# Keeping the last two steps' rows on chip and loading Toeplitz rows by halves, in a GRU, convolution and MoE kernel

## The chip, the cores and the metric

The kernel runs on one core of one Trainium2 chip. The metric is the device time of one execution in microseconds, as the median of several runs. The engines are named as in the profile: PE (TensorE, with PEld for its weight loads), DVE (VectorE), ACT (ScalarE), POOL (GpSimd), and SP (SyncE), whose work here is to issue DMAs. PEq, SPq, ACTq and POOLq are the queues in which an engine's instructions wait to be issued.

## The reference, cut to what matters

`x` is 128 x 64 x 512 (batch, steps, features), `cond` 128 x 512, all float32. Two layers change `x` one after the other:

```
# layer 0
h = cond
for t in range(64):                       # GRU over the 64 steps, state 512
    r, z = sigmoid(...), sigmoid(...)
    n = tanh(i_n + r * h_n)
    h = (1 - z) * n + z * h
    hs[:, t] = h
x = x + hs @ ternary(weight).T + bias     # BitLinear: sign matrix times one scale

# layer 1
w = cond[:, None, :]                      # 128 taps for each of the 512 features
y = depthwise_causal_conv(x, w) + b       # y[b, t, d] = sum over s <= t of x[b, s, d] * w[127 - (t - s), d]
y = moe(y) + shared_expert(y)             # 64 experts, top 6, plus a SwiGLU of width 704
x = x + y
```

Because the 64 steps are shorter than the 128 taps, the convolution of one feature `d` is a product of the 128 x 64 matrix of its inputs with a 64 x 64 triangular Toeplitz matrix of taps.

## The kernel before, in words

The work is written with a framework in which pools of tiles share on-chip memory. A new tile waits for whatever still uses the memory it takes. Each engine and each queue runs its instructions in the order in which the framework arranged them, and `tc.issue_after(i)` asks that what is issued in its block on the engine of `i` comes behind `i`.

**GRU stage (0 to 1405 us).** Step `t` runs 12 matmuls of 512 columns (L480) with the gates on DVE and ACT. Between them PE does the input gates two steps ahead (L326) and `ffn(t - 1)` (L398), the BitLinear product of the step before. `ffn` writes `x1` (L413), the row block of one output step, and stores it twice: into `x1c` (L415), the convolution's input in DRAM, arranged by feature, and into `out` (L428). The last two steps (`TAIL = 2`) are not stored into `x1c`; zeros stand there. Their part of the convolution, which concerns only the last two output steps, is computed on DVE by `tail_products` (L551) from `xl` (the two rows, loaded again from `out`, L546) and `tap` (the last two rows of `cond`), and added at L583. In steps 2 to 33 `toeplitz` (L129) writes the Toeplitz rows of 16 features at a time from the array `taps` into DRAM (`tzd`), each a window of 64 taps.

**Convolution stage (1405 to 1500 us).** It has 16 slices (`NSL`) of 32 features. For a slice, `load_piece` (L147) loads `xc` (1 MB: partitions are 2 feature halves x 64 steps) and two `tz` tiles of 256 KB (`load_toeplitz`, L141; one on SP's queue, one on ACT's for most slices). There are four buffers (`NCB`), so slice `n + 4` is loaded when slice `n` has been multiplied. `clear` (L118) zeroes on POOL the blocks of `tz` that belong to the other feature half. `conv_group` (L163) multiplies four features: `parts=2` splits the 128 batch rows in two halves of 64 columns of the array, `parts=1` takes all 128 at once. A slice has four groups. The four groups of slice 0 are issued early (L512 to L520), around the last transposes and the last `ffn`, into the memory banks psx, psy, psw, psz; the other slices use four banks psc. DVE adds the bias and writes `hid` (L571), 64 tiles of 128 x 512 that stay on chip, two instructions for a group. `hid` takes over the memory of the GRU stage's tiles. Rows 0 to 3 of `hid` are stored into the table `tab` (L590) in two portions, after slice 13 and after slice 15, because the next stage transposes them in place.

**First MoE block (from 1500 us).** The weights of the shared expert (`gw`, `swr`, `swg`, `swu`, L612 to L621) are loaded on SP's queue into the memory of the convolution's buffers. `put_rows` (L1007) stores further rows of `hid` into `tab`. `route(0)` (L940) transposes rows 0 to 3 on PE (L947), copies them back in place (L948) and computes the logits. `shared(0)` (L821) forms the sums `s1`, `s2` on DVE (L830, L831) and runs seven products for each block of 128 columns (L664) after Winograd's variant of Strassen's scheme; `prepare_shared(c)` (L627) makes the weights' sums that products 5 and 6 need (psz and y at L664). The rest of the time (1519 to 2697 us) goes to the other 15 blocks and to the routed experts.

Of the kernel before, what the change touches and what calls it, by code (L numbers as in the profile page):

```python
# [42 lines left out]
def adaln_ffn_kernel(  # L43
# [30 lines left out]
    tzd = dram.tile([2 * NSL, T, DS, T], F32, name="tzd")  # L74
# [23 lines left out]
    def load_rows(dst, src):  # L98

        nc.sync.dma_start(out=dst, in_=src.rearrange("(k p) n -> p k n", p=P))  # L100
# [9 lines left out]
    def conv_buffers(i):  # L110
        cv = conv.enter_context(
            tc.tile_pool(name=f"cv{i}", bufs=1, side="right", reuse_waits="tile")
        )
        tz = cv.tile([P, 2, DS, T], F32, name=f"tz{i}")
        tzs.append(tz)
        xcs.append(cv.tile([P, B, DS], F32, name=f"xc{i}"))

    def clear(i):  # L118
        for hf in range(2):
            nc.gpsimd.memset(tzs[i][hf * T : (hf + 1) * T, 1 - hf], 0.0)  # L120

# [6 lines left out]

    def toeplitz(q):  # L129

        i = nc.sync.dma_start(
            out=tzd[q],
            in_=bass.AP(taps.tensor, taps.offset + q * DS * 2 * T, [[1, T], [2 * T, DS], [1, T]]),
        )
        tc.keep_in_program_order(i)

        nc.sync.dma_start(
            out=x1c[q, :TAIL].rearrange("s (r b) e -> (s r) (b e)", r=8), in_=zrow[: 8 * TAIL, : B * DS // 8]
        )

    def load_toeplitz(sl):  # L141

        for hf, queue in enumerate((nc.sync, nc.sync if 2 <= sl < NCB else nc.scalar)):
            queue.dma_start(out=tzs[sl % NCB][hf * T : (hf + 1) * T, hf], in_=tzd[2 * sl + hf])

    TAIL = 2
    def load_piece(sl):  # L147
        load_toeplitz(sl)
        nc.sync.dma_start(
            out=xcs[sl % NCB], in_=x1c[2 * sl : 2 * sl + 2].rearrange("h s b e -> (h s) b e")  # L150
        )
# [11 lines left out]
    def conv_group(sl, g, ps, parts=2):  # L163


        ps = ps.rearrange("p (j h t) -> p j h t", j=4, h=2)
        for j in range(4):
            for r in range(parts):
                rows = slice(r * B // parts, (r + 1) * B // parts)
                i = nc.tensor.matmul(  # L170
                    ps[rows, j],
                    xcs[sl % NCB][:, rows, g * 4 + j],
                    tzs[sl % NCB][:, :, g * 4 + j, :],
                    start=True,
                    stop=True,
                )
        grouped.append(i)
        return ps
# [9 lines left out]
    with (  # L188
# [96 lines left out]
        gis = {}  # L285
# [112 lines left out]
        def ffn(t, pieces):  # L398
# [13 lines left out]
            x1 = io0.tile([P, D], F32, name="x1")  # L412
# [48 lines left out]
        for t in range(T):  # L461
# [9 lines left out]
            if t == T - TAIL:  # L471
                wi_.close()
                for i in range(2, NCB):
                    conv_buffers(i)
                    clear(i)
            ps_g = []
# [35 lines left out]
        early = [conv_group(0, 0, ps_gi.tile([P, D], F32, name="psx"), 1)]  # L512
        with tc.issue_after(grouped[-1].ins):
            turned = turned_up(h)
        early.append(conv_group(0, 1, ps_gi.tile([P, D], F32, name="psy"), 1))
# [3 lines left out]
        early.append(conv_group(0, 2, ps_gi.tile([P, D], F32, name="psw"), 1))  # L519
        early.append(conv_group(0, 3, ps_gi.tile([P, D], F32, name="psz")))  # L520
# [21 lines left out]


    tail = conv.enter_context(tc.tile_pool(name="tail", bufs=1, reuse_waits="tile"))
    xl = tail.tile([P, TAIL, D], F32, name="xl")
    nc.gpsimd.dma_start(out=xl, in_=out_t[T - TAIL :].rearrange("t b d -> b t d"))  # L546
    tap = tail.tile([P, TAIL, D], F32, name="tap")
    for j in range(TAIL):
        nc.gpsimd.dma_start(out=tap[:, j], in_=cond[B - 1 - j].partition_broadcast(P))
# [7 lines left out]

    cb_h = cb.rearrange("p (q h d) -> p q h d", h=2, d=DS)
    with tc.tile_pool(name="ps_c", bufs=4, space=PSUM) as ps_c:
        for sl in range(NSL):  # L560

            if sl >= NCB:
                load_piece(sl)
            for g in range(DS // 4):
                if early:
                    ps = early.pop(0)
                else:
                    ps = conv_group(sl, g, ps_c.tile([P, D], F32, name="psc"))
                d = slice(g * 4, g * 4 + 4)
                for th in range(2):  # L570
                    nc.vector.tensor_tensor(  # L571
                        hids[th][:, :, 2 * DS * sl : 2 * DS * (sl + 1)].rearrange(
                            "p t (h d) -> p t h d", h=2
                        )[:, :, :, d],
                        ps[:, :, :, th * TH : (th + 1) * TH].rearrange("p j h t -> p t h j"),
                        cb_h[:, sl, :, d].unsqueeze(1).to_broadcast([P, TH, 2, 4]),
                        ALU.add,
                    )
            if sl >= NCB:
                if sl == NCB:  # L580
                    tail_products()
                d = slice(0 if sl == NCB else 2 * DS * sl, 2 * DS * (sl + 1))
                nc.vector.tensor_add(  # L583
                    hids[1][:, TH - TAIL :, d], hids[1][:, TH - TAIL :, d], xl[:, :, d]
                )

            if sl in (NSL - 3, NSL - 1):
                d = slice(0, 2 * DS * (NSL - 2)) if sl == NSL - 3 else slice(2 * DS * (NSL - 2), D)
                for t in range(4):
                    nc.sync.dma_start(out=tab_t[t, :, d], in_=hid(t)[:, d])  # L590
# [30 lines left out]
    load_rows(swu, sw_up[:, : full * P])  # L621
# [5 lines left out]
    def prepare_shared(c):  # L627
# [8 lines left out]
        nc.vector.tensor_sub(t4, w21, t2)  # L636

    NB = 4
    NI = T // NB
# [10 lines left out]
    def winograd(n, accs, lhs, rhs, k0=0):  # L650
# [11 lines left out]
        for k in range(HK):  # L662
            r = rhs(k)
            nc.tensor.matmul(  # L664
# [6 lines left out]
            )  # L671
        return ps
# [148 lines left out]
    def shared(i, sums=None):  # L821
# [8 lines left out]
        nc.vector.tensor_add(s1, x21, x22)  # L830
        nc.vector.tensor_sub(s2, s1, x11)  # L831
        if i == 0:
            prepare_shared(0)
# [13 lines left out]
        for p in range(2):  # L847
            sg = sh.tile([P, QT], F32, name=f"g{p + 1}")
            nc.scalar.activation(sg[rest:], gu[:rest, p * QT : (p + 1) * QT], AF.Silu)
            for j in range(2):  # L850
                nc.vector.tensor_mul(
                    aTr[j * rest : (j + 1) * rest, p],
                    sg[rest:, j * P : (j + 1) * P],
                    gu[rest:, p * QT + j * P : p * QT + (j + 1) * P],
                )
# [7 lines left out]
        for c in range(full):  # L863
            cur = Block(c, ops, aT)
            for n in (1, 6, 7, 3, 2, 4, 5):
                which = prev if n == 3 else cur
                if which:
                    which.product(n)
# [65 lines left out]
    with (  # L934
# [5 lines left out]
        def route(i):  # L940


            for j in range(NB):
                t = i * NB + j
                ps = ps_t1.tile([P, KD, P], F32, name="pst1")
                for k in range(KD):
                    nc.tensor.transpose(ps[:, k, :], hid(t)[:, k * P : (k + 1) * P], ident)  # L947
                nc.vector.tensor_copy(hid(t).rearrange("p (k b) -> p k b", k=KD), ps)  # L948
# [58 lines left out]
        def put_rows(i):  # L1007
            if i < NI:
                for t in range(i * NB, i * NB + NB):
                    nc.sync.dma_start(out=tab_t[t, :, :D], in_=hid(t))  # L1010
# [9 lines left out]
        for _ in range(NB + 1):  # L1020
            next(ahead)
        for i in range(NI // 2):
# [3 lines left out]
            def routing():  # L1026
                if i == 0:
                    yield from ahead
                for r in (2 * i + 1, 2 * i + 2):
                    if r < NI:  # L1030
                        yield from route(r)
# [3 lines left out]
            for n, _ in enumerate(shared(i)):  # L1035
                if done * PIECES <= n * 16:
                    next(routing_, None)
# [384 lines left out]
```

## Time and profile before

| what | value |
|---|---|
| median of 3 runs | 2700.56 us (2699.63 to 2701.82) |
| profiled execution | 2699.08 us |
| its span in the profile | 2697.0 us |
| PE busy in the span | 2647.6 us (98%) |
| mean granted clock of PE | 0.997 |
| GRU stage | 0 to 1405 us, PE busy 1394.08 |
| convolution | 1405 to 1500 us, PE busy 72.63 |
| first MoE block, to its regular pace | 1500 to 1519 us, PE busy 14.95 |
| rest | 1519 to 2697 us, PE busy 1165.96 |

The profile is one execution. Its waits view sums the idle time of an engine by what ended it. The timeline merges instructions of one kind in order of time and gives in brackets the idle time before them. The windows view gives for a stretch of time the busy time and number of instructions of PE, PEld, DVE, ACT and POOL, then the clock granted to PE (1.00 is full speed), the share of the DMA engines that is busy, and the rate in GB/s. A float32 matmul appears as two records.

### The profile page before, as it was taken

How to read it: one execution, taken by the hardware profiler on the slowest of the kernel's cores; microseconds unless marked ns; L12 is line 12 of the kernel's file. 1: busy time of each engine (PE TensorE's matmuls, PEld its weight loads, DVE VectorE, ACT ScalarE, POOL GpSimd, SP SyncE). 2: the span in 40 equal slices, each digit the busy share in tenths (PEclk: the TensorE clock that was granted, in tenths of full speed). 3: DMA queues.
4: the chain of work that ended last, by engine and by line, in shares of the span. 5: the costliest groups of instructions: out<-in, count | busy, mean ns of one | idle time of the engine just before them, and what ended most of it. 6: DMA issues, size and time to landing. Idle time of an engine off the chain costs nothing. (4 is left out here: it accounts for less than half of the span.)

```text
span 2697.0 us, 31139 instructions
## 1 busy us (share of the span) xinstructions
PE 2647.6 (98%) x11935; PEld 1825.2 (68%) x11935; DVE 1414.2 (52%) x3148; ACT 426.1 (16%) x794; POOL 425.2 (16%) x475
## 2 busy tenths in 40 slices
PE   8999999999999999999997899999999999999999
PEld 5666666666666666666667766777777666666667
DVE  6555555555555555555546655555665333433334
ACT  1111111111111111111110222222221111111111
POOL 2111111111111111111110000000001222222220
PEclk9999999999999999999999999999999999999999
DMA  5333223232222222322249631222255999998962
GB/s 191 74 61 72 61 62 63 55 63 55 63 47 57 50 50 51 66 51 43 44 98 274 244 117 22 39 56 57 62 151 166 288 306 287 303 317 267 297 186 47
DMA packets 459588, 328.04 MB, mean 122 GB/s; under 512 B 312304, under 2 KB 378864, under 8 KB 457264
## 3 DMA queue, kind: packets, MB, share of 16 engines
q1 hardware_dynamic: 432336, 255.52, 34.0%
q0 software_dynamic: 25984, 66.86, 10.5%
q10 hardware_dynamic: 1120, 3.67, 0.6%
q8 instruction: 94, 1.54, 0.2%
q14 instruction: 54, 0.44, 0.1%
HBM read 239.73 MB, written 94.65 MB: 124 GB/s over the span
## 5 line engine op out<-in xcount | busy, mean ns | idle before, releaser
L480 PE MATMUL psgh<-whh,hT 128*128 128x512 f32 x1536 | 674.5, 595 | 0.7 <-ACT hT L387 0.7
L480 PEld LDWEIGHTS psgh<-whh,hT 128*128 128x128 f32 x1536 | 286.8, 190 | 349.8 <-issue 336.0
L326 PE MATMUL psx<-wih,xp 128*128 128x256 f32 x768 | 198.8, 381 | 6.2 <-DMA wih<-in_w_ih_dram 6.2
L208 POOL DMA_DIRECT2D xn<-in_x_dram x61 | 33.9, 555 | 838.2 <-DVE x L413 826.6
L326 PEld LDWEIGHTS psx<-wih,xp 128*128 128x128 f32 x768 | 143.9, 191 | 25.8 <-issue 6.2
L490 DVE TENSOR_TENSOR n<-psgh,bhn 128x512 f32<-128x512 f32 x64 | 44.3, 692 | 175.2 <-PE psgh L480 175.2
L1294 DVE SCALAR_TENSOR_TENSOR a<-a,rw,pu 128x352 f32<-128x352 f32 x32 | 18.6, 580 | 215.1 <-PE pu L1285 208.5
L387 ACT COPY hT<-psf 128x512 f32<-128x512 f32 x64 | 37.4, 585 | 583.7 <-PE psf L381 583.7
L487 DVE TENSOR_TENSOR r<-psgh,gi 128x512 f32<-128x512 f32 x64 | 44.3, 692 | 141.1 <-PE psgh L480 141.1
L401 POOL TENSOR_TENSOR xn<-xn,fb 128x512 f32<-128x512 f32 x64 | 80.7, 1263 | 145.1 <-DMA xn<-in_x_dram 145.1
L326 PE MATMUL psz<-wih,xs 128*128 128x256 f32 x384 | 98.7, 379 | 1.8 <-DVE gi L349 1.8
L326 PE MATMUL psy<-t,xs 128*128 128x256 f32 x384 | 99.9, 383 | 0.3 <-DVE t L277 0.2
L326 PE MATMUL psw<-wih,xp 128*128 128x256 f32 x384 | 99.7, 381 | 0.0
L326 PE MATMUL psw<-t,xp 128*128 128x256 f32 x384 | 99.0, 380 | 0.2 <-DVE u L347 0.2
L326 PE MATMUL psz<-t,xs 128*128 128x256 f32 x384 | 98.7, 379 | 0.0
L405 PE MATMUL psf<-sgn,hhi 128*128 128x512 f32 x256 | 95.1, 493 | 0.0
L1311 PE MATMUL py<-wd,aeT 128*64 128x512 f32 (+1 forms) x384 | 89.5, 601 | 0.0
L341 DVE TENSOR_TENSOR p<-psx,bi 128x512 f32<-128x512 f32 x96 | 66.4, 692 | 37.3 <-PE psx L326 37.0
L664 PE MATMUL psx<-hid,swg 128*128 128x256 f32 x320 | 83.8, 384 | 0.2 <-DMA swg<-in_sw_gate_dram 0.2
L170 PE MATMUL psc<-tz,xc 128*64 128x128 f32 x960 | 62.9, 294 | 21.4 <-DMA xc<-x1c 13.3
L664 PE MATMUL psx<-xr,swg 128*128 128x256 f32 x320 | 83.6, 383 | 0.0
L493 ACT ACTIVATE n<-n 128x512 f32<-128x512 f32 x64 | 40.3, 629 | 274.0 <-DVE n L492 274.0
(298 smaller groups left out, 4669.2 us busy)
## 6 DMA issues: line engine op xcount, KB each, us to landing
wg<-in_w_gate_dram SPq DMA_DIRECT2D x64, 704.0 KB
wu<-in_w_up_dram SPq DMA_DIRECT2D x64, 704.0 KB
wd<-in_w_down_dram SPq DMA_DIRECT2D x64, 512.0 KB
x1c<-x SPq DMA_DIRECT2D x62, 256.0 KB
out_dram<-x SPq DMA_DIRECT2D x62, 256.0 KB
xn<-in_x_dram POOLq DMA_DIRECT2D x61, 256.0 KB, 4.1
xp<-in_xT_dram POOLq DMA_DIRECT2D x30, 512.0 KB, 5.5
tab<-hid SPq DMA_DIRECT2D x60, 256.0 KB
```

The source lines that it names most:

```text
L170: i = nc.tensor.matmul(ps[rows, j], xcs[sl % NCB][:, rows, g * 4 + j], tzs[sl % NCB][:, :, g * 4 + j, :], start=True, stop=True,)
L326: i = nc.tensor.matmul(ps, self.ops[n][:, k, :], self.ws[n][:, k, :], start=(first and k == 0), stop=(k == HK - 1), skip_group_check=not f ...
L341: add(self.p1, both, b)
L387: nc.scalar.copy(hT, ps)
L401: nc.gpsimd.tensor_add(xn, xn, fb)
L405: nc.tensor.matmul(ps, piece[:, k, :], sgn[:, k, :], start=(i == 0 and k == 0), stop=(i == 1 and k == KD - 1),)
L480: nc.tensor.matmul(ps, hT[:, k, :], whh[c][:, k, :], start=(k == 0), stop=(k == KD - 1))
L487: nc.vector.tensor_add(r, ps_r, gis.pop((t, 0)))
L490: nc.vector.tensor_add(n, ps_n, bhn)
L493: nc.scalar.activation(n, n, AF.Tanh)
L664: nc.tensor.matmul(ps.rearrange("p (j b) -> p j b", b=P) if len(r.shape) == 3 else ps, lhs(k), r, start=(first and k == 0), stop=(k == HK ...
L1311: nc.tensor.matmul(py[halves[j]], self.aeT[:n, c, halves[j]], self.ws[j][2][:n, c, :], start=(c == 0), stop=(c == len(ech) - 1),)
```

## The change

The last two `x1` are written straight into `xl`, a tile that is opened together with `tap` before the last two steps, in memory of its own at the other end; nothing is loaded back from `out`. The Toeplitz rows are kept by halves of the 64 output steps: for output steps 0 to 31 only input rows 32 to 63 (in the reversed order in which they are stored) can be other than zero, so that half is 32 rows, and the rest is zeroed once on POOL. All groups of slice 0 are computed in halves of 64 columns, and x, y and w are issued before the last transposes. The stores of rows 0 to 3 move: the first portion behind the load of slice 15 on SP's queue, the second to ACT's queue. In the first MoE block the rows' stores are issued behind the shared weights, those of rows 4 to 7 on POOL's queue, and the order of DVE's and PE's first instructions is laid down: copies of rows 0 to 3, `prepare_shared(0)`, `s1` and `s2`, then the rest; rows 4 and 5 are transposed before the logits.

```
-    tzd = dram.tile([2 * NSL, T, DS, T], F32, name="tzd")
+    tzd = dram.tile([2 * NSL, 2, T, DS, T // 2], F32, name="tzd")
...
-        tz = cv.tile([P, 2, DS, T], F32, name=f"tz{i}")
+        tz = cv.tile([P, 2, 2, DS, T // 2], F32, name=f"tz{i}")
...
             nc.gpsimd.memset(tzs[i][hf * T : (hf + 1) * T, 1 - hf], 0.0)
+            nc.gpsimd.memset(tzs[i][hf * T : hf * T + T // 2, hf, 0], 0.0)
...
+    HALVES = [(0, T // 2), (1, 0)]
     def toeplitz(q):
+        for u, s0 in HALVES:
+            i = nc.sync.dma_start(
+                out=tzd[q, u, s0:],
+                in_=bass.AP(
+                    taps.tensor,
+                    taps.offset + q * DS * 2 * T + s0 + u * T // 2,
+                    [[1, T - s0], [2 * T, DS], [1, T // 2]],
+                ),
+            )
+            tc.keep_in_program_order(i)
...
-            queue.dma_start(out=tzs[sl % NCB][hf * T : (hf + 1) * T, hf], in_=tzd[2 * sl + hf])
+            for u, s0 in HALVES:
+                queue.dma_start(
+                    out=tzs[sl % NCB][hf * T + s0 : (hf + 1) * T, hf, u], in_=tzd[2 * sl + hf, u, s0:]
+                )
...
-    def conv_group(sl, g, ps, parts=2):
+    def conv_group(sl, g, ps):
...
-                    ps[rows, j],
+                    ps[rows, j].rearrange("p h (u t) -> p h u t", u=2),
                     xcs[sl % NCB][:, rows, g * 4 + j],
-                    tzs[sl % NCB][:, :, g * 4 + j, :],
+                    tzs[sl % NCB][:, :, :, g * 4 + j, :],
...
-            x1 = io0.tile([P, D], F32, name="x1")
+            if t < T - TAIL:
+                x1 = io0.tile([P, D], F32, name="x1")
+            else:
+                x1 = last[0][:, t - (T - TAIL)]
...
+                tail = conv.enter_context(
+                    tc.tile_pool(name="tail", bufs=1, side="right", reuse_waits="tile")
+                )
+                xl = tail.tile([P, TAIL, D], F32, name="xl")
+                tap = tail.tile([P, TAIL, D], F32, name="tap")
+                for j in range(TAIL):
+                    nc.gpsimd.dma_start(out=tap[:, j], in_=cond[B - 1 - j].partition_broadcast(P))
+                last += [xl, tap]
...
-        early = [conv_group(0, 0, ps_gi.tile([P, D], F32, name="psx"), 1)]
+        early = [
+            conv_group(0, g, ps_gi.tile([P, D], F32, name=f"ps{n}")) for g, n in enumerate("xyw")
+        ]
         with tc.issue_after(grouped[-1].ins):
             turned = turned_up(h)
-        early.append(conv_group(0, 1, ps_gi.tile([P, D], F32, name="psy"), 1))
+        early.append(conv_group(0, 3, ps_gi.tile([P, D], F32, name="psz")))
...
-    nc.gpsimd.dma_start(out=xl, in_=out_t[T - TAIL :].rearrange("t b d -> b t d"))
...
+            if sl == NSL - 1:
+                store_first(slice(0, 2 * DS * (NSL - 2)), nc.sync)
...
-            if sl in (NSL - 3, NSL - 1):
-                d = slice(0, 2 * DS * (NSL - 2)) if sl == NSL - 3 else slice(2 * DS * (NSL - 2), D)
-                for t in range(4):
-                    nc.sync.dma_start(out=tab_t[t, :, d], in_=hid(t)[:, d])
+            if sl == NSL - 1:
+                store_first(slice(2 * DS * (NSL - 2), D), nc.scalar)
...
+        with behind(marks, i == 0):
+            nc.vector.tensor_add(s1, x21, x22)
+        marks.append(nc.vector.tensor_sub(s2, s1, x11))
-        if i == 0:
-            prepare_shared(0)
...
+                    with behind(products, i == 0 and c < 2):
+                        which.product(n)
...
-                for t in range(i * NB, i * NB + NB):
-                    nc.sync.dma_start(out=tab_t[t, :, :D], in_=hid(t))
+                with tc.issue_after(loaded.ins):
+                    for t in range(i * NB, i * NB + NB):
+                        (nc.gpsimd if i == 1 else nc.sync).dma_start(
+                            out=tab_t[t, :, :D], in_=hid(t)
+                        )
...
         ahead = route(0)
-        for _ in range(NB + 1):
+        for _ in range(NB):
+            next(ahead)
+        with tc.issue_after(marks[-1].ins):
+            marks.append(prepare_shared(0))
+        second = {}
+        for t in (NB, NB + 1):
+            second[t], last = turn(t)
+        with tc.issue_after(last.ins):
             next(ahead)
```

`loaded` is the load of `swu`, and `turn(t)` the four transposes of one row. `store_first` stores the given columns of rows 0 to 3:

```
+    def store_first(d, queue):
+        for t in range(4):
+            queue.dma_start(out=tab_t[t, :, d], in_=hid(t)[:, d])
```

## The prediction

> **What bounds the kernel now.** I read the page first. Its busy row says that TensorE works nearly throughout, so what is to be gained by moving work about is the rest of the span, 2697.0 - 2647.6 = 49.4 us, plus time in which PE is busy but slow.
>
> ```profile
> span 2697.0 us, 31139 instructions
> PE 2647.6 (98%) x11935; PEld 1825.2 (68%) x11935; DVE 1414.2 (52%) x3148; ACT 426.1 (16%) x794; POOL 425.2 (16%) x475
> ```
>
> The waits of PE, asked for 1400 to 1520 us, where the convolution (L170) and the first MoE block lie, hold about half of it:
>
> ```profile
> PE psc L170 <- DMA xc<-x1c: 13.3, 7, 3.5
> PE psc L170 <- DVE hid L571: 4.6, 1, 4.6
> PE psc L170 <- issue: 3.3, 1, 3.3
> PE psz L664 <- DVE st L633: 2.8, 1, 2.8
> ```
>
> The timeline of PE gives the places (start, duration, instruction, idle before):
>
> ```profile
> 1405.38 1.80 PE L170 MATMUL psx<-tz,xc 128*128 128x128 f32 x8
> 1411.04 0.94 PE L170 MATMUL psz<-tz,xc 128*64 128x128 f32 x10
> 1414.94 3.91 PE L170 MATMUL psc<-tz,xc 128*64 128x128 f32 x64 [0.23 <-DVE x L413]
> 1423.43 25.49 PE L170 MATMUL psc<-tz,xc 128*64 128x128 f32 x384 [4.57 <-DVE hid L571]
> 1451.06 3.96 PE L170 MATMUL psc<-tz,xc 128*64 128x128 f32 x64 [2.13 <-DMA xc<-x1c]
> ...
> 1486.05 4.00 PE L170 MATMUL psc<-tz,xc 128*64 128x128 f32 x64 [0.23 <-DMA xc<-x1c]
> 1493.53 5.54 PE L170 MATMUL psc<-tz,xc 128*64 128x128 f32 x64 [3.48 <-DMA xc<-x1c]
> ...
> 1514.54 1.97 PE L664 MATMUL psz<-space,st 128*128 128x256 f32 x4 [2.79 <-DVE st L633]
> ```
>
> One of the 16 slices is 64 records and costs PE 4.0 us, of which the weight loads fill nearly all (PEld under psc is busy 61.3 us beside PE's 62.9). From slice 8 on, slices start 5.83 us apart: (1486.05 - 1451.06) / 6. Two windows of 4 us say what sets that pace (last two columns: DMA share, GB/s):
>
> ```profile
> 1424.00:1428.00 4.00, 4.00 (x42) 4.00 (x40) 2.34 (x7) 0.00 (x0) 0.00 (x0) 0.50 0.97 363
> 1472.00:1476.00 4.00, 2.61 (x46) 2.42 (x42) 3.13 (x9) 0.00 (x0) 0.00 (x0) 1.00 0.99 267
> ```
>
> The DMA engines are full at 267 GB/s while PE idles: a slice brings 1 MB of xc and two tz of 256 KB, 1.573 MB, which in 5.83 us is 270 GB/s. The first window shows the clock column at 0.50 behind the 4.57 us stall. DVE and SP show what began the two long stalls:
>
> ```profile
> 1421.43 0.42 DVE L571 TENSOR_TENSOR hid<-psx,cb 128x256 f32<-128x256 f32 x1 [3.92 <-DMA out_dram<-x]
> 1474.64 0.45 SPq L144 DMA_DIRECT2D tz<-tzd  x1
> 1486.44 1.81 SPq L590 DMA_DIRECT2D tab<-hid  x4
> 1488.29 0.46 SPq L149 DMA_DIRECT2D xc<-x1c  x1
> 1499.57 1.74 SPq L590 DMA_DIRECT2D tab<-hid  x4
> 1503.49 0.51 SPq L100 DMA_DIRECT2D swu<-in_sw_up_dram  x1
> ```
>
> The evictions into the upper half of hid wait for the store of the last x1, whose memory hid takes over. The xc of slice 15 stands in SP's queue behind four tab stores that wait for slice 13's evictions. And swg and swu are issued only behind the stores of slice 15; DVE's L633 then waits for swu until 1514.06.
>
> **The change part by part.** The sums are made on the profiled execution: 2699.08 us, its span 2697.0. The median of the runs is 1.48 us above it, and I add that at the end.
>
> *GRU stage, costed at nothing.* 32 toeplitz DMAs become 64 (SPq, 0.556 us each: 0.56 us more in a step of 22 us in which SP issues 0.37 + 2.81 + 0.56 us), with 1536 runs of 128 B in place of 1024 of 256 B. The DMA share is 0.30 from 100 to 400 us, with toeplitz, and 0.25 from 800 to 1100, without: 0.05 x 22 = 1.1 us of the engines per step, half as much again afterwards. PE is busy 300.00 of 300 us in both windows; its work covers this. Without that cover the price would be about 0.6 + 0.6 us in 32 steps, 38 us. The loads of slices 0 to 3 go from 8 tz DMAs to 16; the last of them leave SP before 1382 instead of 1379, and SP's next work is at 1391. The added memsets (quarter size; the present ones take 0.945 us for 64x1024, so at most 0.5 us each) end on POOL near 1385; POOL's next work is at 1406.87. The tap loads stay where they ran, at 1382; the xl load (1421.57) is gone.
>
> *Early groups in halves.* x, y and w take 1.8 to 1.9 us as 128 columns each; in halves a group costs a quarter of a slice, 1.0 us. Against this speaks the Trainium skill, TensorEngine Tiling, Key Properties: changing the tiling mode drains the array. The row: psz in halves, 10 records from 1411.04 to 1411.91, 0.87 us where the pace of 4.0 / 64 gives 0.63, so a visit costs 0.25 to 0.3 us. Now there are two visits (psz twice, the second running on into psc), then three: 0.3 more. From 1405.38: x, y, w 3.3, transposes 0.43, z 1.3 (ends 1410.4), psf 2.23 (as 1403.15 to 1405.38), switch 0.3: slice 1 starts at 1412.9, not 1414.94. h is ready at 1407.17, before the transposes. By the rule at its worst, a drain of a microsecond at each switch, the 2.0 us would be gone; by the row they stay.
>
> *The order inside tz.* The moving operand now has four runs of 32 where it had two of 64. No row shows it. It can't be a gain, since the columns are as many; a loss could reach, at most, a doubling of 15 x 4.0 us. Nearest is psc itself, whose pace its weight loads account for: I take 0.
>
> *The last two x1 kept on chip.* L413 of the last step ends near 1413.6, and hid no longer lies on a tile that a DMA still reads. Eight evictions of slice 0 take 8 x 0.33 = 2.7 us, so slice 2 waits some 0.4 us at 1416.9 in place of 4.57, and its clock stays up (slice 2 lasted 6.5 us at 0.50). What is late next is the data. The stores still read xl, and tail_products overwrites it at slice 4 (now 1430): they have landed by then.
>
> *DMA pace.* Slice 4's loads leave at 1410.4 instead of 1414.75 and are in by 1418; slice 5's leave when slice 1 ends, 1416.9, and flow from 1418.2 (before, 1414.75 to traffic near 1416 shows this delay). From here the DMA engines are the bound: slices 2 and 3 free their buffers by 1426, sooner than the engines get to slices 6 and 7. A slice is now 1024 + 2 x 192 KB = 1.442 MB, 0.917 of before. By bytes that is 5.34 us. The low end is the tz share: the best windows with few tz loads reach 350 to 363 GB/s, so xc alone is 3.0 us and tz the other 2.8; a quarter less is 5.1. The high end: rows of 2 KB instead of 4 and five DMAs for three keep it at 5.83 or 6.5. I take 5.34.
>
> Here the Trainium skill speaks against the change: DMA: Bandwidth & Descriptors, Bandwidth and "Anatomy of one DMA", gives about 2.0 us fixed plus bytes / 436 GB/s for a transfer, and asks for 1 MB or more in each. Two more per slice would cost up to 4 us less 0.3. But the same fit, one after the other, makes a slice of before 3 x 2.0 + 3.6 = 9.6 us, and the trace shows 5.83: with several in flight the fixed parts overlap. I go by the trace. By the rule a slice would take 5.34 + 4 = 9.3 us.
>
> *End of the convolution.* 11 slices from 1418.2: 1418.2 + 58.7 = 1476.9, 0.5 to the first matmul, 4.0 of PE: 1481.4 against 1499.07 (1493.53 + 5.54). That is 17.7 us. In it is that slice 15's xc no longer stands behind the tab stores, worth 3.5 us of idle and 1.5 of low clock. The stores go behind it in SP's queue, 0.92 MB, 3.3 us of DMA time before the weights.
>
> *First MoE block.* gw, swr, swg and swu (3 MB) no longer stand behind slice 15's stores, which move to ACT's queue (0.45 us each; ACT is next needed for the logits, 5 us later). They leave about 5 us before the convolution ends; with the stores ahead and put_rows(1) (1 MB, now POOL's queue, 4 x 0.88 us of it) beside them, at the 390 GB/s of 1508 to 1516, swu is in 7 to 9 us after that end, where it was 15. DVE runs prepare_shared(0) (4 x 0.42) and then s1 and s2 before they are wanted, 11.6 us after the end. So the 2.79 us go, and psz and y cost 0.87 each again, not 1.77 and 1.70 (clock 0.50 behind the stall): 1.7. New: DVE is now queued behind swu, its sums with it, and the first copy waits for ACT's store of hid(0) to be read, with weight traffic beside it (before, the copy came 1.55 us after the store's issue). Between 0 and 2 us; I take 0.5. Net 4.0 us.
>
> Sum: 17.7 + 4.0 = 21.7 us off 2699.08 is 2677.4; plus 1.48, 2678.9 us. PE's listed waits after 1530 come to 7.3 us, none of them for a DMA, so the shift reaches the end in full.
>
> **The rivals.** (a) PE becomes the bound, if tz was what made the traffic slow and a slice falls to 4.8 us or less: convolution to 1412.9 + 0.4 + 15 x 4.0 = 1473.3, and the block's stall fully gone (4.5): 25.8 + 4.5 = 30.3 off, 2670. For: 363 GB/s in a good window. Against: 13 windows at 1.0 share and 278 on average.
> (b) The split gains nothing on the DMA side, 5.83 to 6.5 us a slice: end at 1486.8 to 1494.2, 12.3 to 4.9 off, the block 2 to 4 more: 2684 to 2694. For: more, shorter rows, and SP already waits for earlier transfers before it issues (tz for an xc: 11.6 us in 3 waits). Against: the expert stage moves rows of 1.4 KB at 279 GB/s in the mean.
> (c) Slower: the five transfers of a slice queue on each other's completion so that fixed times add. It decides from (1499.07 + 4.0 - 4.5 - 1418.2) / 11 = 7.3 us a slice; at 9.3 the convolution ends at 1525.0, 26 later, less 4: 2722 us.
> (d) The change does not free the evictions: hid waits for some other tile of the stage (xn, hlo). Then slice 2 keeps part of its 4.57 us and low clock; slice 6's load leaves 4 to 5 us later and the DMA engines idle for about 3: 2682.
>
> **How the numbers follow.** Main case 0.60, range of its own 2673 to 2684 (5.1 to 5.6 us a slice, block 2.5 to 5). (a) 0.14, (b) 0.17, (c) 0.04, (d) 0.05. The range 2668 to 2688 holds the main case, (a), (d) and half of (b). A measurement of this kernel can tell about 0.2%, 5.4 us: faster than that 0.94, within it 0.03 (the far end of (b), and (c) near its point of decision), slower 0.03.
>
> **What would show it.** Right: L571's wait on out_dram gone and no stretch at clock 0.50 near 1424; slices starting 5.1 to 5.6 us apart with DMA share near 1; slice 15's xc issued as soon as slice 11 ends; the last psc ending near 1481; L633 without a wait of over 1 us. Wrong: slices 4.0 apart without idle (a), 5.8 or more (b), over 7.3 (c); psc records slower than 4.0 us per 64; a long wait of L948 for a store, or of L633 for swu, that takes back the block's 4 us.

## The result and the profile after

The changed kernel takes 2688.09 us (median of 6 runs, 2682.18 to 2690.43) against 2699.43 us of the kernel before on the same chip: ratio 0.9954, 95% interval 0.9942 to 0.9967. It is faster, as forecast, but by half: 11 us, where 21.7 were worked out, and 0.09 us beyond the slow end of the range. Its profiled execution took 2688.51 us, with a span of 2686.1 (before 2699.08 and 2697.0). The page of after:

```profile
span 2686.1 us, 31288 instructions
PE 2642.5 (98%) x11959; PEld 1818.0 (68%) x11959; DVE 1413.3 (53%) x3148; ACT 426.1 (16%) x794; POOL 430.4 (16%) x486
```

PE's waits from 1400 to 1520 us (total, times, longest):

```profile
PE psc L184 <- DMA xc<-x1c: 5.3, 4, 1.9
PE psc L184 <- DMA tz<-tzd: 3.1, 2, 1.6
PE pst L981 <- DVE hid L991: 2.7, 1, 2.7
PE y L694 <- DVE space L863: 2.4, 1, 2.4
```

The 13.3 us for xc have become 5.3, with 3.1 for tz beside them, the 4.6 for L571 are gone, and so is the 2.8 of psz for st. In their place stand two waits of the first MoE block: the transposes wait 2.7 us for a copy (L991; before, 1.0 us in two waits), and a product waits for the sums (L863), which it did not before. The timeline of PE in after shows where:

```profile
1394.16 12.26 PE L507 MATMUL psgh<-whh,hT 128*128 128x512 f32 x24 [0.67 <-ACT hT L401]
1408.20 1.20 PE L184 MATMUL psx<-tz,xc 128*64 128x128 f32 x16
...
1416.32 22.60 PE L184 MATMUL psc<-tz,xc 128*64 128x128 f32 x384 [0.91 <-DVE xl L430]
1440.87 3.94 PE L184 MATMUL psc<-tz,xc 128*64 128x128 f32 x64 [1.96 <-issue]
...
1473.40 3.98 PE L184 MATMUL psc<-tz,xc 128*64 128x128 f32 x64 [1.94 <-DMA xc<-x1c]
1478.07 7.66 PE L184 MATMUL psc<-tz,xc 128*64 128x128 f32 x128 [0.69 <-DMA xc<-x1c]
1486.69 1.07 PE L981 MATMUL pst<-ident,hid 128*128 128x128 f32 x8 [0.95 <-DVE hid L598]
1487.59 1.04 PE L981 MATMUL y<-ident,hid 128*128 128x128 f32 x8
1491.28 1.27 PE L981 MATMUL pst<-ident,hid 128*128 128x128 f32 x8 [2.66 <-DVE hid L991]
...
1502.93 1.13 PE L694 MATMUL y<-space,st 128*128 128x256 f32 x4 [2.37 <-DVE space L863]
1504.28 2.07 PE L694 MATMUL psw<-hid,swu 128*128 128x256 f32 x4 [0.22 <-DVE hid L887]
```

Three stages can be read off such a timeline in every version. S is the start of the first early group (psx, 1408.20; before 1405.38), E the end of the last psc (1478.07 + 7.66 = 1485.73; before 1499.07). The convolution is E - S: 77.5 us, before 93.7. The block is from E to the start of what follows the six products 1, 6, 7, 2, 4, 5 of the first shared column: 24.0 us, before 21.6. Span - E, called the rest below, holds the block and all behind it: 1200.4, before 1197.9, so that behind the block nothing has changed (+2.5 and +2.4). The stages give -16.2 for the convolution, +2.4 for the block, +2.8 for a later S. That is the whole result: the convolution won what was promised, and 5 us were given back at its two sides.

### The profile page after: what moved, and what is told of

The parts are those of the page before. It is cut to its first block, busy times and chain, and to the rows that moved or that the text cites. A ratio compares the mean times of both kernels' runs of the same rounds, so it can differ in the third digit from the quotient of the medians.

```text
span 2686.1 us, 31288 instructions
## 1 busy us (share of the span) xinstructions
PE 2642.5 (98%) x11959; PEld 1818.0 (68%) x11959; DVE 1413.3 (53%) x3148; ACT 426.1 (16%) x794; POOL 430.4 (16%) x486
## 5 line engine op out<-in xcount | busy, mean ns | idle before, releaser
L694 PE MATMUL psx<-xr,swg 128*128 128x256 f32 x320 | 83.6, 383 | 0.0
L358 DVE TENSOR_TENSOR u<-psy,p 128x512 f32<-128x512 f32 x96 | 66.3, 691 | 29.4 <-PE psy L340 29.1
```

The source lines that it names most:

```text
L358: add(self.u2, both, self.p1)
L694: i = nc.tensor.matmul(ps.rearrange("p (j b) -> p j b", b=P) if len(r.shape) == 3 else ps, lhs(k), r, start=(first and k == 0), stop=(k == ...
```

## The experiments

The versions were measured in sets, each beside runs of before, so that the ratios can be compared and the medians only within a set. The stages come from one profiled execution of each version, and they vary by chance too: after and its repetition (e_after), the same program, have blocks of 24.0 and 23.2 and a rest of 1200.4 and 1197.8; before and e_tail, which run the same code behind E, have 21.6 and 19.8, 1197.9 and 1194.8. In e_oldblock, e_oldblock2 and e_quarters the block also holds 0.9 us of later work (the transposes of one more row and half a product).

| version | median us, ratio (95%) | S | conv. | block | rest |
|---|---|---|---|---|---|
| before | 2699.43 | 1405.38 | 93.7 | 21.6 | 1197.9 |
| after | 2688.09, 0.9954 (0.9942-0.9967) | 1408.20 | 77.5 | 24.0 | 1200.4 |
| e_after | 2685.45, 0.9957 (0.9940-0.9973) | 1408.11 | 77.5 | 23.2 | 1197.8 |
| e_tail | 2697.16, 0.9999 (0.9990-1.0007) | 1405.17 | 91.1 | 19.8 | 1194.8 |
| e_fulltz | 2690.47, 0.9972 (0.9960-0.9983) | 1405.56 | 83.6 | 24.4 | 1198.0 |
| e_quarters | 2694.12, 0.9988 (0.9980-0.9997) | 1410.26 | 87.5 | 20.5 | 1195.9 |
| e_notz | 2670.59 (one run) | 1406.84 | 64.0 | 23.2 | 1198.1 |
| e_oldblock | 2681.24, 0.9938 (0.9920-0.9957) | 1406.60 | 77.4 | 20.8 | 1195.7 |
| e_oldblock2 | 2681.99, 0.9952 (0.9935-0.9968) | 1405.56 | 77.0 | 20.8 | 1194.7 |
| e_gwpool | 2687.80, 0.9962 (0.9948-0.9975) | 1406.43 | 78.2 | 24.2 | 1199.3 |
| e_nostore | 2684.64, 0.9956 (0.9939-0.9973) | 1405.92 | 77.5 | 23.8 | 1198.1 |
| e_psync | 2683.14, 0.9951 (0.9935-0.9968) | 1406.73 | 77.8 | 21.7 | 1196.6 |
| e_both | 2682.94, 0.9947 (0.9931-0.9964) | 1410.95 | 77.5 | 21.9 | 1196.9 |
| e_sums | 2682.93, 0.9949 (0.9933-0.9966) | 1408.31 | 77.7 | 18.8 | 1194.1 |

### The convolution: e_tail, e_fulltz, e_quarters, e_notz

e_tail is the kernel before with one part of the change, the last two x1 kept on chip:

```
-            x1 = io0.tile([P, D], F32, name="x1")
+            if t < T - TAIL:
+                x1 = io0.tile([P, D], F32, name="x1")
+            else:
+                x1 = last[0][:, t - (T - TAIL)]
...
```

> The kernel before with one part of the change alone: the last two x1 are written into xl, nothing else. If the traffic of xc and tz bounds the convolution, the 4.57 us stall and the low clock of slice 2 go, but slices 8 to 15 stay 5.8 us apart, and only what the DMA engines idled near 1430 (2 us) and the 0.5 MB of xl (1.7 us) come back: 3 to 5 us less than before. Rival: the stall and the low clock count in full, 7 us or more.

PE's timeline of e_tail:

```profile
1414.75 19.16 PE L170 MATMUL psc<-tz,xc 128*64 128x128 f32 x320 [0.24 <-DVE xl L416]
1435.88 4.05 PE L170 MATMUL psc<-tz,xc 128*64 128x128 f32 x64 [1.97 <-DMA xc<-x1c]
...
1491.13 5.14 PE L170 MATMUL psc<-tz,xc 128*64 128x128 f32 x64 [3.69 <-DMA xc<-x1c]
```

The 4.57 us stall and its low clock are gone (320 records in one piece), yet the convolution is only 2.6 us shorter: the data is late next, and slices 8 to 13 start 6.1 us apart. The time itself cannot be told from before, so the 3 to 5 us that were expected do not show in it.

e_fulltz is the changed kernel with whole Toeplitz rows again:

```
...
-            for u, s0 in HALVES:
-                queue.dma_start(
-                    out=tzs[sl % NCB][hf * T + s0 : (hf + 1) * T, hf, u], in_=tzd[2 * sl + hf, u, s0:]
-                )
+            queue.dma_start(out=tzs[sl % NCB][hf * T : (hf + 1) * T, hf], in_=tzd[2 * sl + hf])
...
```

> The changed kernel with the Toeplitz rows loaded in full (256 KB per tz, three DMAs per slice instead of five), nothing else. If bytes set the pace, slices from 7 on lie 5.8 us apart where the changed kernel has 5.42, and the convolution ends 3 to 4 us later. Rival, the count of transfers sets it: the same pace or a faster one, and the time not longer.

PE's timeline of e_fulltz:

```profile
1439.53 5.56 PE L175 MATMUL psc<-tz,xc 128*64 128x128 f32 x64 [2.76 <-DMA xc<-x1c]
...
1474.90 4.01 PE L175 MATMUL psc<-tz,xc 128*64 128x128 f32 x64 [1.14 <-DMA xc<-x1c]
```

Its slices 7 to 13 start (1474.90 - 1439.53) / 6 = 5.9 us apart; those of after (1473.40 - 1440.87) / 6 = 5.42. The halves are worth 83.6 - 77.5 = 6.1 us of the convolution, and E comes 3.4 us later without them, as expected (the intervals of the two times still touch). What lies between e_tail and e_fulltz, 7.5 us, is the early groups in halves together with slice 15's xc ahead of the tab stores. Such differences of single profiles are good to about a microsecond: the versions with the same code for the convolution have 77.0 to 78.2.

e_quarters (on e_oldblock) goes further the same way: quarters, 320 KB of tz per slice in place of 384, but nine DMAs in place of five.

```
-    HALVES = [(0, T // 2), (1, 0)]
+    HALVES = [(u, T - (u + 1) * T // 4) for u in range(4)]
```

> The kernel of e_oldblock with the Toeplitz rows loaded by quarters of the output steps instead of halves: 160 KB per tz instead of 192, in four DMAs of 1 KB rows, so nine DMAs per slice instead of five. If bytes set the pace, slices from 7 on lie 4.9 to 5.0 us apart instead of 5.4, and the convolution is about 4 us shorter. If the number of transfers in flight or their fixed costs count (the mechanism of the slower rival), the pace is 6 us or more and the convolution longer.

PE's timeline of e_quarters, its waits from 1440 to 1500 us, and a window of it:

```profile
1452.95 5.53 PE L186 MATMUL psc<-tz,xc 128*64 128x128 f32 x64 [3.27 <-DMA tz<-tzd]
...
1485.72 7.59 PE L186 MATMUL psc<-tz,xc 128*64 128x128 f32 x128 [3.05 <-DMA tz<-tzd]
```
```profile
PE psc L186 <- DMA tz<-tzd: 16.8, 7, 3.6
```
```profile
1445.00:1485.00 40.00, 27.45 (x398) 26.28 (x396) 21.12 (x59) 0.00 (x0) 0.00 (x0) 0.91 0.67 216
```

Fewer bytes, and slower: (1485.72 - 1452.95) / 5 = 6.55 us a slice, always waiting for tz, and the convolution 10 us longer. The rows are shorter as well, 1 KB in place of 2, but it is not the DMA engines that are slow: they are busy for 0.67 of the time, where after has 1.00 from 1440 to 1478 us. They lack transfers to work on. The compiled programs show a way: the DMAs of SP and ACT take eight completion semaphores in turn, and each waits for the one eight places ahead, so that nine a slice can not all be under way. S is later too, by 3.7 us against e_oldblock, 2.65 of them where ACT issues four Toeplitz loads in the GRU steps (on that see below, at the GRU stage). That the eight semaphores are the whole of it was not tried.

e_notz is the changed kernel without the Toeplitz loads of slices 4 to 15:

```
-        load_toeplitz(sl)
+        if sl < NCB:
+            load_toeplitz(sl)
```

> The changed kernel without the Toeplitz loads of slices 4 to 15, which then use the rows of slices 0 to 3 (the convolution of these 12 slices is not the right one). A slice brings 1.05 MB of xc alone. If bytes set the pace of 5.42 us a slice, xc alone at 270 to 360 GB/s takes 2.9 to 3.9 us, PE becomes the bound at 4.0 us a slice and the convolution from the first early group on falls from 77.5 to 67 to 69 us. Rival: the pace is that of the xc load by itself (rows of 8 KB from 128 places, one transfer that waits for a free buffer and for the earlier one); then slices stay 5 us or more apart and the convolution at 74 to 77.

PE's timeline of e_notz, one line for 15 slices:

```profile
1414.95 55.90 PE L185 MATMUL psc<-tz,xc 128*64 128x128 f32 x960 [0.91 <-DVE xl L431]
```

No wait is left. PE needs 55.90 / 15 = 3.73 us a slice, and the convolution takes 64.0 us, 3 less than expected. In after the Toeplitz traffic, 27% of the bytes, therefore still costs 13.5 us. The rival, that the xc load sets the pace, falls.

### The block: what gave the gain back

e_oldblock keeps the change but gives the first MoE block its order of before, with put_rows on SP alone. e_oldblock2 is the same kernel once more.

```
-        with behind(marks, i == 0):
-            nc.vector.tensor_add(s1, x21, x22)
-        marks.append(nc.vector.tensor_sub(s2, s1, x11))
+        nc.vector.tensor_add(s1, x21, x22)
+        nc.vector.tensor_sub(s2, s1, x11)
+        if i == 0:
+            prepare_shared(0)
...
-        with tc.issue_after(marks[-1].ins):
-            marks.append(prepare_shared(0))
...
-                with tc.issue_after(loaded.ins):
...
-                        (nc.gpsimd if i == 1 else nc.sync).dma_start(
```

> The changed kernel with the first MoE block in the order of before (sums before prepare_shared(0), no order laid down for PE and DVE, put_rows on SP); the stores of slice 15 stay on ACT's queue. If the new order of DVE (s1 and s2 behind the sums that need swu) is what the block lost, the time from the last psc to the end of product 4, 5, 6, 7 and the second product 1 or 2 falls from 24.0 us back to 19 to 22 us, and the kernel is 2 to 5 us faster than the changed one. If what counts is that swu is issued late, since it waits for the completion of a store of ACT's queue, this kernel has the same wait, and the block stays at 22 to 25 us.

> The changed kernel with the first MoE block in its order of before, once more, beside the two others. If its lead over the changed kernel (0.9938 against 0.9954 to 0.9957) is real, 0.993 to 0.9945 again with a block of 20 to 20.5 us; if it was chance, 0.995 to 0.996.

The block falls to 20.8 us in both, against 24.0 and 23.2 in after and e_after: the new order and queues cost some 3 us. DVE and PE of e_oldblock:

```profile
1487.13 1.29 DVE L991 COPY hid<-pst 128x512 f32<-128x512 f32 x2 [2.12 <-DMA tab<-hid]
1499.14 0.76 DVE L658 TENSOR_TENSOR st<-swu,swg 128x256 f32<-128x256 f32 x2
1499.62 1.13 PE L694 MATMUL psz<-space,st 128*128 128x256 f32 x4 [0.33 <-DVE st L658]
```

The weights' sums (L658) are no earlier than anywhere else, 15.2 us after E, but only psz needs them there, and it waits 0.33 us. The first copy waits 2.12 us. The same rows of DVE in after, with s1 (L862) and SP's two big weight loads:

```profile
1490.54 1.30 DVE L991 COPY hid<-pst 128x512 f32<-128x512 f32 x2 [3.74 <-DMA tab<-hid]
1499.57 0.76 DVE L658 TENSOR_TENSOR st<-swu,swg 128x256 f32<-128x256 f32 x2 [5.72 <-DMA tab<-hid]
1501.26 0.68 DVE L862 TENSOR_TENSOR space<-hid 128x512 f32<-128x512 f32 x1
1483.56 0.86 SPq L101 DMA_DIRECT2D swg<-in_sw_gate_dram  x1
1490.43 0.37 SPq L101 DMA_DIRECT2D swu<-in_sw_up_dram  x1
```

And ACT of after, with the longest wait of SP from 1470 to 1530 us:

```profile
1486.38 1.87 ACTq L580 DMA_DIRECT2D tab<-hid  x4
```
```profile
SPq L101 <- DMA tab<-hid: 6.9, 3, 6.0
```

The first copy overwrites hid(0), so it waits until ACT's store has read it: issued at 1486.38, copy at 1490.54, 4.2 us, while swg is under way beside it (389 GB/s from 1488 to 1492). swu leaves SP only at 1490.43, 4.7 us after E and 6.0 after SP was done with swg: it takes its turn on the semaphore of ACT's first store. This is SP's end of the compiled program of after, with what each DMA waits for (the store carries DMAHW6):

```
SP   DMACopy swg<-in_sw_gate_dram 128x4x640 [waits DMAHW5_49]
SP   DMACopy swu<-in_sw_up_dram 128x4x640 [waits DMAHW6_49]
ACT  DMACopy tab<-hid 128x64 [waits DVE_49,DMAHW6_49,Activation_49,Pool_49]
```

swu is usable at 1499.57, 13.8 us after E (L658 is put down to a tab store in the row, but it reads swg and swu). L658 to L661 and then s1, s2 (L862, L863) stand behind it on DVE, and y needs s1 and s2: 2.37 us, with PE's next two products at a low clock (psw 2.07 us where 1.03 is usual; the clock is 0.50 from 1504.3 to 1506.2).

e_gwpool puts gw and swr on GpSimd's queue, so that swu's turn is no longer on that semaphore:

```
-    load_rows(gw, gateT)
+    load_rows(gw, gateT, nc.gpsimd)        # the two swr loads likewise
```

> The changed kernel with three small loads (gw and the two swr) issued on POOL's queue instead of SP's. Nothing else moves, but swu is then no longer the eighth DMA behind the first store of ACT's queue, so it needn't wait for that store's completion. If this wait is why swu left at 1490.4, 4.7 us after the last psc, it now leaves before the last psc ends, L658 starts 8 to 10 us after that end instead of 13.8, PE's wait for L863 (2.4 us) and the low clock behind it (1.8 us) go: 3 to 5 us faster than the changed kernel. Rival, the DMA engines are simply full: swu lands as late as before the move, and the time is the same within 1 us.

DVE and SP of e_gwpool:

```profile
1491.11 0.69 DVE L991 COPY hid<-pst 128x512 f32<-128x512 f32 x1 [5.39 <-DMA tab<-hid]
1494.48 0.75 DVE L658 TENSOR_TENSOR st<-swu,swg 128x256 f32<-128x256 f32 x2
1481.32 0.38 SPq L101 DMA_DIRECT2D swu<-in_sw_up_dram  x1
```

swu leaves 3.3 us before E, 8 us earlier than in after, and nothing waits for it any more. But now swg and swu both lie beside ACT's stores (1485.29), with GpSimd's small loads behind them, and the first copy waits until 1491.11. The block stays at 24.2. The time is that of after, as the rival had it, but not for the rival's reason, since swu is in time (L658 at E + 9.8).

e_nostore is the reverse. ACT's stores behind slice 15 (the last 64 columns of rows 0 to 3, those of slices 14 and 15) are left out; as many bytes, from the 64 columns before, are sent ahead by SP.

```
                 store_first(slice(0, 2 * DS * (NSL - 2)), nc.sync)
+                for t in range(4):
+                    nc.sync.dma_start(out=tab_t[t, :, D - 64 : D], in_=hid(t)[:, D - 128 : D - 64])
...
-            if sl == NSL - 1:
-                store_first(slice(2 * DS * (NSL - 2), D), nc.scalar)
```

> The changed kernel without the stores of rows 0 to 3 behind slice 15 (the last 64 columns of these rows in the table are filled early from the neighbouring columns, so the table holds wrong values there). Neither the first copy nor swu then waits for a store that is issued after the last eviction. If these stores are what the block lost, the first copy follows the first transposes within 1 us, PE has no wait over 1 us before the first product, and the block is 6 to 8 us shorter than the changed kernel's (16 to 18 us). Rival: swu, moved by the full DMA engines, comes too late in any case, and the block is at most 3 us shorter.

DVE and PE of e_nostore:

```profile
1485.02 1.29 DVE L990 COPY hid<-pst 128x512 f32<-128x512 f32 x2 [0.55 <-PE pst L980]
1497.20 0.76 DVE L657 TENSOR_TENSOR st<-swu,swg 128x256 f32<-128x256 f32 x2 [9.70 <-DMA swu<-in_sw_up_dram]
1500.55 2.08 PE L693 MATMUL y<-space,st 128*128 128x256 f32 x4 [6.34 <-DVE space L862]
```

The copies run at once, and all of it is lost at y: 6.34 us. swu was issued at 1484.02, 0.6 us after E where after has 4.7, and yet DVE has it only at 1497.20, 13.8 us after E as in after. The rival held: swu is late although nothing holds its issue. From 1484.0 to 1497.2 the DMA engines are full (share 0.99, 349 GB/s, or 4.6 MB, of which swu is 1.3), so other transfers take the time: swg, swd, and the rows on POOL's and SP's queues. The next run moves the rows on POOL's queue.

e_psync puts put_rows(1) on SP, behind swu:

```
-                        (nc.gpsimd if i == 1 else nc.sync).dma_start(
+                        nc.sync.dma_start(
```

> The changed kernel with put_rows(1) on SP's queue, behind swu, instead of POOL's. If the first copy waits because the small stores of rows 0 to 3 share the DMA engines with the weights and with POOL's 1 MB, the stores land a microsecond or so sooner (about 3 us from issue instead of 4) and swu lands 2 to 3 us sooner: the block is 1 to 3 us shorter than the changed kernel's. If POOL's stores have no part in it, the block is as long as before the move.

swu is usable at E + 11.7 in place of 13.8, y waits 0.79 us instead of 2.37, the first copy still 4.04; the block is 21.7. So POOL's 1 MB delayed swu and not the copies. e_after is after unchanged, beside these:

> The changed kernel as it is, beside the others on one chip: 2686 to 2689 us; the block from the last psc to the end of product 5 of the first column block 23 to 25 us, the first copy L991 over 3 us after the last psc's eviction.

PE's timeline of e_after:

```profile
1491.34 1.97 PE L981 MATMUL pst<-ident,hid 128*128 128x128 f32 x8 [2.91 <-DVE hid L991]
1493.24 3.85 PE L1002 MATMUL lg<-hid,gw 128*64 128x256 f32 x16
...
1502.15 1.13 PE L694 MATMUL y<-space,st 128*128 128x256 f32 x4 [0.18 <-DVE space L863]
```

The block is 23.2 us and swu is usable at E + 13.2, but y waits only 0.18 us. The clock fell already behind the wait for the copy (0.50 from 1491.3 to 1497.0), so PE came to y later by itself. Where the loss appears, as a wait of y or as slow matmuls before it, differs between two executions of one program; swu is late in both. Against e_after the gain of e_psync is 1.5 us, and against after 2.3.

e_both joins e_gwpool and e_nostore (both diffs above):

> The changed kernel with both edits at once: gw and swr loaded on GpSimd's queue, so that swu does not stand eight DMAs behind ScalarE's first store, and the stores of slice 15's 64 columns left out for rows 0 to 3 (the last 64 columns of these rows of the table are then not the final ones). If the block lost its gain to two gates in series (the copies behind the stores, then DVE's sums behind swu), and each of the two edits alone only bared the other, both together bring the block from 23 to 24 us down to 17 to 20 and the time to 0.993 to 0.994 of the kernel before. Rival: swu is late whatever is done, because 3 MB of weights and 1 MB of put_rows share the DMA engines from the end of the convolution on; swu then lands 12 to 14 us after that end, DVE's sums with it, and the block stays at 22 us or more, the time at 0.995 to 0.996.

PE's timeline of e_both:

```profile
1491.15 1.04 PE L980 MATMUL pst<-ident,hid 128*128 128x128 f32 x8
1496.66 3.40 PE L1001 MATMUL lg<-hid,gw 128*64 128x256 f32 x16 [4.47 <-DMA gw<-in_gateT_dram]
```

Neither pst nor y waits, yet the block is 21.9, near the rival's 22. It does not decide between them: gw, issued at 1490.00 on POOL's queue behind the first of its put_rows, is now what comes late, a wait that the edit made itself. What the rival said of swu did not hold here: it is usable at E + 10.1, not 12 to 14. e_sums therefore leaves the loads as in e_psync and takes only DVE's sums out from behind swu:

```
         marks.append(nc.vector.tensor_sub(s2, s1, x11))
+        if i == 0:
+            marks.append(prepare_shared(0))
...
-        with tc.issue_after(marks[-1].ins):
-            marks.append(prepare_shared(0))
```

> The changed kernel with put_rows(1) on SP's queue and s1, s2 put ahead of prepare_shared(0) on DVE again; the turned rows and the two-queue stores stay. If DVE's sums behind swu are what is left of the block's loss, it falls from the 21.7 us of the version with put_rows(1) on SP alone to about 20.3, as in the old block order, and the time to about 0.994. If the wait of the first copies (4.0 us there) is what is left, it stays at 21.5 to 22 and 0.995.

DVE and PE of e_sums:

```profile
1490.90 1.29 DVE L993 COPY hid<-pst 128x512 f32<-128x512 f32 x2 [3.83 <-DMA tab<-hid]
1493.48 0.69 DVE L862 TENSOR_TENSOR space<-hid 128x512 f32<-128x512 f32 x1
1494.20 0.69 DVE L863 TENSOR_TENSOR space<-space,hid 128x512 f32<-128x512 f32 x1
1497.94 0.75 DVE L658 TENSOR_TENSOR st<-swu,swg 128x256 f32<-128x256 f32 x2
1499.93 1.03 PE L694 MATMUL y<-space,st 128*128 128x256 f32 x4
```

The sums are done at 1494.9, y does not wait, and L658 starts when DVE is free. The block is 18.8 us, the shortest of all and under the 20.3 expected, though the first copy still waits 3.83. The last column of the table leans the same way: the five versions of the changed or half-changed kernel with the sums ahead of swu (e_tail, e_quarters, both e_oldblock, e_sums) have a rest of 1194.1 to 1195.9, those with the sums behind it 1196.6 to 1200.4. But before, which has the sums ahead as well, has 1197.9, 3.1 more than e_tail with the same code, so this column alone shows nothing. e_oldblock and e_sums (ratios 0.9938, 0.9952, 0.9949) are ahead of after and e_after (0.9954, 0.9957) in the medians, and are the versions to keep, but the intervals overlap: it is the stage that shows the lead, not the total.

## Why the prediction was half right

**The convolution: right.** Forecast 1405.38 to 1481.4, 76.0 us; measured 77.5. Each term answers. L571's wait is gone; slice 2 has neither gap nor low clock (1.00 from 1416 to 1439 us). The pace by bytes, 5.34 us, came out at 5.42, and the halves by themselves at 6.1 us, where 11 x (5.83 - 5.34) = 5.4 was counted. Early groups and store order together measured 7.5, forecast 2.0 + 5.0. The early part alone (psx to the first psc) went from 9.56 to 8.12 us, 1.4 and not 2.0, since slice 1 now waits 0.91 us for the last x1 (L430). No switch of the tiling mode cost a microsecond, a price that no row gave: psz in halves takes 1.21 us where 22.60 / 24 = 0.94 is a quarter of a slice, so about 0.27 for a visit, as read from before. The order inside tz cost nothing: six slices take 22.60 us, and 23.02 with whole rows (e_fulltz).

**The rivals.** (a) failed: PE waits before every slice from 7 to 14. What it would have been is e_notz. (b) was refuted by 5.42 and by e_fulltz. (c), transfers queueing on each other's completion, costs nothing at five DMAs a slice, where the engines stay full; e_quarters shows that it is real at nine, still under the 7.3 us of its point of decision. The rule weighed there, the Trainium skill's fixed 2.0 us for each transfer (DMA: Bandwidth & Descriptors, Anatomy of one DMA), would have given an estimated 9.3 us, and 5.42 were measured. The page fits that figure to transfers that GpSimd issues; these are issued by SP and ACT. The trace was the better guide to the size, but it could not say at what count more transfers begin to cost. (d) failed with L571's wait.

**The block: the step that failed.** "Between 0 and 2 us; I take 0.5. Net 4.0 us" was forecast as a gain; measured is a loss of 2.4, 6.4 us off and the largest error. (By e_after it is a loss of 1.6.) Two terms were mis-sized. The wait of the first copy was taken from the 1.55 us between a store that landed alone and the copy, which in before waits for PE and not for the store:

```profile
1501.12 1.29 DVE L948 COPY hid<-pst 128x512 f32<-128x512 f32 x2 [0.98 <-PE pst L947]
```

So the 1.55 us bound the store's time from above, and say nothing of a store with company. Beside swg it took 4.2 from issue, and PE lost 2.66 us. And swu "in 7 to 9 us after that end" came at 13.8. That step summed bytes at 390 GB/s and missed that swu's issue waits its turn behind ACT's store; but e_nostore, with the issue at E + 0.6, is no earlier, so the bytes in front of it and beside it were undercounted as well (4.6 MB in that time, at 349 GB/s). The queue that the prediction itself named, DVE's sums behind swu, was then costed inside those 0.5 us: e_sums shows it at 21.7 - 18.8 = 2.9 us, from one profile of each version. Mechanism seen, price wrong.

**The GRU stage: costed at nothing, cost about 1 us.** The last step's psgh group starts at 1392.9 to 1393.2 in the three versions with whole rows (before, e_tail, e_fulltz), and at 1393.2 to 1396.9, median 1394.2, in the ten with halves. PE's cover holds nearly everything of the 38 us it was said to hide, but not all, and what it lets through is not on SP's queue, the one the prediction counted, but on ACT's. ACT in before, then in after:

```profile
142.04 0.45 ACTq L144 DMA_DIRECT2D tz<-tzd  x1
142.53 0.58 ACT L387 COPY hT<-psf 128x512 f32<-128x512 f32 x1 [9.53 <-PE psf L381]
```
```profile
142.14 1.34 ACTq L155 DMA_DIRECT2D tz<-tzd  x2
143.52 0.58 ACT L401 COPY hT<-psf 128x512 f32<-128x512 f32 x1 [10.18 <-DMA tzd<-in_taps_dram]
```

Here, and once before at 98 us, ACT issues two Toeplitz loads where it issued one; here, by the bracket, it also waits for Toeplitz rows that are still being written. It copies hT, which the next psgh group needs, only behind them, and PE waits for the copy:

```profile
144.16 10.57 PE L507 MATMUL psgh<-whh,hT 128*128 128x512 f32 x24 [0.51 <-ACT hT L401]
```

From the psgh group at 77 us to the one at 165 us the three versions with whole rows take 86.9 to 87.0 us, the ten with halves 87.6 to 87.9, and e_quarters, with four loads, 90.3. From there to the group at 773 us all take 608.2 to 608.5, so that the Toeplitz DMAs of SP, which go on until 748 us, cost nothing. The rest of the spread is older: the group at 57 us starts anywhere from 56.3 to 59.3.

The other 1.7 us by which S is late in after are a low clock in that one last group: 12.26 us for 24 records, 10.57 in before and in e_oldblock2 (clock 0.86 from 1394 to 1406 us, and 1.00 in e_oldblock2). It comes in some profiles and not in others of the same GRU code, and its cause stays open.

The sum: 2.8 (S) + 1.5 (convolution) + 6.4 (block) + 0.1 (after it) + 0.3 (around the span) = 11.1, which is 2688.5 - 2677.4.

## What to carry to other kernels

When a stage is sped up by bytes, count the DMAs as well, and look at what stands behind them on every queue that issues them: halves of a triangle paid, quarters lost more than they saved. When a load is moved ahead of stores, follow it past what it lands beside and past what its consumer's engine has queued behind it: sums that need no weights belong in front of those that do. Removing one of two waits in series moves the loss to the other, so change the order on the engine where both meet before changing the transfers.

## What was not expected of the hardware

A store of 128 x 256 B freed its source within 1.55 us of issue when it ran alone, after about 2.5 in e_oldblock (weights issued behind it), 4.2 in after (beside swg) and 5.8 in e_gwpool (beside swg and swu). Nine DMAs a slice moved fewer bytes more slowly than five, 6.55 us against 5.42, with the DMA engines a third idle. Without gaps a slice costs PE 3.73 to 3.77 us with halves, and 3.83 or 3.84 with whole rows (e_tail, e_fulltz), and not the 4.0 that one slice by itself shows.
